# Cross attention and mixture of experts on one core: the first block only centred, its root applied behind its product, and the zero fill on ScalarE

## The chip, the cores and the metric

The kernel runs on 1 core of a Trainium2 chip. The metric is the time of one execution on the device in microseconds; of several runs the median counts. Engines are named as in the profile: PE (TensorE matmul), PEld (its weight load), DVE (VectorE), ACT (ScalarE), POOL (GpSimd), SP (SyncE).

## The reference

Input `x` has 4 x 512 = 2048 tokens of 512 values. A layernorm is followed by a first stage in which each token is sent, by its token number, to one of four context matrices; a second layernorm is followed by a mixture of 32 experts with top 4 routing and a shared expert. All is float32. What the change touches lies in the first stage:

```python
x = x + xattn(_layernorm(x), itok, ctx, ctx, ctx)
# _layernorm: (x - mean) / sqrt(var + 1e-5)
# xattn, for each of the experts e = 0..3, for the tokens whose number falls to e:
g = silu(einsum('bsd,fd->bsf', h, ctx[e]))
u = einsum('bsd,fd->bsf', h, ctx[e])
y = einsum('bsf,df->bsd', g * u, ctx[e].T)
x = x + ffn(_layernorm(x), ...)     # rmsnorm, 32 experts of 256, top 4, and a shared one
```

The three context matrices of one expert are one and the same array, so with p = h times the matrix, the gated value is silu(p) * p.

## The kernel before

**Sorting.** The tokens are sorted by expert on the chip. One-hot products on PE count and rank them (L221 to L265); `xtok` (L265) holds the token number of each sorted place. From then on work goes by blocks of 128 sorted tokens: 16 blocks of rows (`NT`), and 19 visits (`XB`), since a block that straddles two experts is visited for each. `be_i` and `bl_i` hold expert and block of each visit as integers that engines load into registers (`value_load`), `valid` masks the rows of a visit that belong to its expert.

**The plan of the first stage (`xattn`).** Each visit b goes through these steps:

- `x_block(j)` (L331): POOL requests the 128 rows of a block by an indirect DMA into `acc[:, j, :]`. These requests and the roots stand on POOL in one written order (`in_turn`).
- `x_moments` (L342, L344, L345): DVE takes mean and variance (`st`, `xmv`).
- `x_root` (L348, L351, L352): DVE adds epsilon (`ve`), POOL raises it to the power -0.5 (`xr`).
- `x_norm` (L401): DVE makes scale and bias (`rv`, L407 and L410), ACT writes the normalised rows `hn` (L426). For block 0, DVE writes the first half of the columns (L416) and ACT the second.
- `turn_block` (L438): PE transposes `hn` into `tp`, and a copy brings it to `xT` (L456 on DVE; for block 0 in halves, the first on ACT and the second on DVE, L446).
- `hold` (L385): ACT copies the visit's context matrix out of `cT` into `held`, two copies of 1024 columns (L395). Visit 0 always has expert 0 and uses `cT[:, 0]` directly.
- `up` (L459): PE forms the transposed product `pp`, 16 products of 128 columns, which the trace lists as 32 instructions (L464). For block 0 they run by input chunk c on the outside, so that they can start with the first half of `xT`.
- `gate` (L476): ACT takes silu (L478), DVE multiplies it by the product (`made`, L480) into `aT`.
- `down` (L482): PE multiplies `aT` by the same matrix, four products of 512 columns, listed as 8 instructions (L485); DVE adds the result to `acc` (L500).

`settle`, `norm` and `turn_row` then start the second layernorm of blocks that are finished; routing and the scatter of rows to `s_dram` by POOL (L652) follow, then the shared expert and the 32 experts.

**What sets the order.** A scheduler orders the instructions of each engine; `behind(a, b)` puts a behind b on its engine (with `Sync`, also behind b's end on another engine), `tc.issue_after` does it for a group. In `xattn`, rows of blocks 0, 1 and 2 are requested at once, those of block 3 behind the root of block 0, those of block 4 behind the root of block 1, and so on; blocks 8 to 15 are requested in a row behind the common root of blocks 4 to 7. `second_inputs` (norm weights, gate, shared expert, zeros for the padding rows of the output) is issued by SP when the statistics of block 7 are done, and `blanks` fills `s_dram` with zeros behind the last request.

**The head.** SP loads `tok_sb` and the first three context matrices of 1 MB (`cT`); the fourth is requested when the plan of the visits is complete (`planned`, L313). DVE makes the constants, among them `ident` (L154). POOL makes the index ramps and fills `none`, 128 x 2084 values, with zeros (L163). `turn_over(n, after_)` puts n products on PE whose results nobody reads: ten behind `xtok`, five behind the statistics of block 0.

Of the kernel before, what the change touches and what calls it, by code (L numbers as in the profile page):

```python
# [17 lines left out]
P = 128  # L18
T = 2048
D = 512  # L20
DC = D // P
GT = 4
G = T // (GT * P)
EX = 4
NT = T // P
# [41 lines left out]
def tile_xattn_moe(  # L67
# [92 lines left out]
    iota_e = const_iota([P, E], [[1, E]], "iota_e")  # L160

    spare = const_iota([P, NT, K], [[K * P, NT], [P, K]], "spare", base=NS, channel=1)
    nc.gpsimd.memset(none, 0.0)  # L163
# [203 lines left out]
    def x_registers(b):  # L367


        if b == 0:  # L370
            off[0] = 0
            regs[0] = 0, 0
            return None
        with queued(downs[-1] if downs else None):

            off[b] = nc.tensor.value_load(be_i[0:1, b : b + 1], min_val=0, max_val=min(b, EX - 1))
        with queued(adds_x[-1] if adds_x else halves[-1] if halves else None):
            dv = nc.vector.value_load(bl_i[0:1, b : b + 1], min_val=0, max_val=NT - 1)
            loaded = nc.cur_bb.bb.instructions[-1]
        with queued(reads[-1] if reads else None):  # L380
            ac = nc.scalar.value_load(bl_i[0:1, b : b + 1], min_val=0, max_val=NT - 1)
        regs[b] = dv, ac
        return loaded

    def hold(b):  # L385

        if b == 0:
            held[0] = cT[:, 0]
            return
        with queued(copies[-1] if copies else None):  # L390
            e = nc.scalar.value_load(be_i[0:1, b : b + 1], min_val=0, max_val=min(b, EX - 1))
        held[b] = ctx_pool.tile([P, DC, D], F32, tag="held", name=f"held{b}", bufs=2)
        n = DC // 2
        for h in range(0, DC, n):
            ins = nc.scalar.copy(  # L395
                held[b][:, h : h + n], cT[:, bass.ds(e, 1), h : h + n].rearrange("p o c f -> p (o c) f")
            )
            apart(ins, matrices[b + 1 :], "of experts that come later")
            copies.append(ins)

    def x_norm(b):  # L401
# [5 lines left out]
        ins = nc.vector.tensor_tensor(rv[:, 0:1], xr[:, bass.ds(dv, 1)], valid[:, b : b + 1], ALU.mult)  # L407
        apart(ins, [q for q in roots[b + 1 :] if q not in roots[: b + 1]], "of blocks that come later")
        powers.append(ins)
        scaled = nc.vector.scalar_tensor_tensor(  # L410
            rv[:, 1:2], xmv[:, bass.ds(dv, 1), 0], -1.0, rv[:, 0:1], ALU.mult, ALU.mult
        )
        hn_[b] = xpool.tile([P, D], F32, tag="hn", name="hn")
        n = D // 2 if b == 0 else 0
        if n:
            scaled = nc.vector.tensor_scalar(  # L416
                hn_[b][:, :n],
                acc[:, bass.ds(dv, 1), :n].rearrange("p o d -> p (o d)"),
                rv[:, 0:1],
                rv[:, 1:2],  # L420
                ALU.mult,
                ALU.add,
            )
            apart(scaled, loads[b + 1 :], "of blocks that come later")
            halves.append(scaled)
        ins = nc.scalar.activation(  # L426
            hn_[b][:, n:],
            acc[:, bass.ds(ac, 1), n:].rearrange("p o d -> p (o d)"),
            AF.Identity,
            bias=rv[:, 1:2],  # L430
            scale=rv[:, 0:1],
        )
        apart(ins, fronts, "of blocks that are done")
        apart(ins, loads[b + 1 :], "of blocks that come later")
        reads.append(ins)
        return scaled

    def turn_block(src, tag, name, eng, after_=None):  # L438
        t = xpool.tile([P, DC, P], F32, tag=tag, name=name)
        if eng is None:  # L440
            n, copies = DC // 2, []
            for h, copy in ((0, nc.scalar.copy), (n, nc.vector.tensor_copy)):
                tp = ps_t.tile([P, n, P], F32, tag="tp", name="tp")
                for c in range(n):
                    ins = nc.tensor.transpose(tp[:, c, :], src[:, (h + c) * P : (h + c + 1) * P], ident)
                copies.append(copy(t[:, h : h + n, :], tp))  # L446
            turns.append(ins)
            turned.append(copies[1])
            return t, copies[0]
# [6 lines left out]
        turned.append(nc.scalar.copy(t, tp) if eng is nc.scalar else nc.vector.tensor_copy(t, tp))  # L456
        return t

    def up(b, fs, after_=None):  # L459
        if fs[0] == 0:  # L460
            ups[b] = ps_m.tile([P, DC, P], F32, tag="mm", name="pp")
        pairs = [(f, c) for f in fs for c in range(DC)] if b else [(f, c) for c in fs for f in range(DC)]
        for f, c in pairs:
            ins = nc.tensor.matmul(  # L464
                ups[b][:, f, :],
                held[b][:, c, f * P : (f + 1) * P],
                xT_[b][:, c, :],
                start=(f == 0 and c == 0) if b == 0 else (c == 0),
                stop=(c == DC - 1),
                skip_group_check=(b == 0),  # L470
            )
            if after_ is not None:
                behind(ins, after_)
        ups_.append(ins)

    def gate(b):  # L476
        s = xpool.tile([P, DC, P], F32, tag="s", name="s")
        gated.append(nc.scalar.activation(s, ups[b], AF.Silu))  # L478
        aT_[b] = xpool.tile([P, DC, P], F32, tag="aT", name="aT")
        made[b] = nc.vector.tensor_tensor(aT_[b], s, ups[b], ALU.mult)  # L480

    def down(b):  # L482
        po = ps_o.tile([P, D], F32, tag="po", name="po")
# [21 lines left out]
    def xattn():  # L505
        def fetched(*js):
            for j in js:
                x_block(j)

        fetched(0, 1, 2)  # L510
        for b in range(2):
            loaded = x_registers(b)
            with tc.issue_after(loaded) if loaded is not None else nullcontext():
                st = x_moments(b)
            behind(st, scaled if b else planned)
            if not b:
                turn_over(5, st)
            x_root(b)
            fetched(3 + b)
            scaled = x_norm(b)  # L520
            if b:
                behind(reads[-1], half_)
            else:
                xT_[0], half_ = turn_block(hn_[0], "xT", "xT", None)
        hold(0)
        up(0, range(DC - 1))
        hold(1)
        xT_[1] = turn_block(hn_[1], "xT", "xT", nc.vector, ups_[0])
        up(0, range(DC - 1, DC), turns[-1])
        gate(0)  # L530
        hold(2)
        for b in range(2, GT):
            st = x_moments(b)
            behind(st, turned[b - 2])
            behind(st, scaled)
            x_root(b)
            fetched(3 + b)
        fetched(GT + 3)
        x_norm(2)
        behind(powers[-1], turned[1])  # L540
        for b in range(XB):
            j = GT * (b // 2 + 1)
            if not b:
                behind(x_moments(GT), made[0])
                x_moments(GT + 1)
            elif j < NT and b % 2 == 0:
                for i in range(j, j + GT):
                    x_moments(i)
                x_root(j, GT)
# [5 lines left out]
                hold(b + 2)  # L555
            if b + 1 < XB:
                up(b + 1, range(DC // 2))

            g, i = divmod(b - (XB - NT) - GT - 2, GT)
            if i == 0 and g >= 0:  # L560
                choose(g, ups_[-1])
            if b + 1 < XB:
                up(b + 1, range(DC // 2, DC))
                gate(b + 1)
                if not b:
                    behind(reads[-1], gated[-1])
            n = b - (XB - NT) - 2
            if n >= 0:
                row_ = turn_row(n, ups_[-1])
            if b + 2 < XB:  # L570
                xT_[b + 2] = turn_block(hn_[b + 2], "xT", "xT", nc.vector)
            if not b:
                for i in range(GT + 2, 2 * GT):
                    st = x_moments(i)
                    behind(st, turned[-1])
                x_root(GT, GT)
                fetched(*range(2 * GT, NT))
                second_inputs(st)
                blanks(loads[-1])
# [826 lines left out]
```

## Time and profile before

| What | Value |
|---|---|
| median of 3 runs | 634.53 us (633.66 to 635.23) |
| profiled execution, its own time | 634.66 us |
| its span, first to last instruction | 632.8 us |
| mean granted TensorE clock | 0.990 |
| busy PE / DVE / POOL / ACT | 606.6 / 396.8 / 249.6 / 216.6 us |
| rows requested by POOL, first and last of 16 | 10.06 and 40.81 us |
| first transposes of block 0 on PE | 16.38 us |
| product of block 1 on PE | 21.84 us |
| first `down` on PE | 25.95 us |

Times inside the profile are counted from the start of the span. The page of the profile gives busy time by engine, the span in 40 slices, the chain of work that ended last and the costliest groups. Of the other views, the timeline lists instructions in order of time, merged where alike, with the idle time ahead of them in square brackets and what ended it; the chain of waits lists start, length and holder of each piece of the chain that ended last; the windows give busy time by engine, granted clock and DMA in chosen stretches.

### The profile page before, as it was taken

Reading aid. Unit: us, or ns where it says so; the run is one execution under the profiler, and the core shown is the slowest. Engines: PE = TensorE matmul, PEld = TensorE weight load, DVE = VectorE, ACT = ScalarE, POOL = GpSimd, SP = SyncE. Lnnn points to the kernel's source line nnn. Section 1 sums busy time; section 2 is a strip of 40 time slices with the busy share of each in tenths; the row PEclk is TensorE's granted clock in tenths of the full one; section 3 lists DMA queues with packets and bytes.
Section 4 is the critical chain, followed back from the end, with each engine's and each line's share of the span. In section 5 each row is a group of like instructions: output and inputs, shape, how many; then the busy total and the mean of one; then the engine's idle time right before and its main releaser. Section 6 shows DMA issues by size and latency. Waiting matters only on the chain.

```text
span 632.8 us, 10430 instructions
## 1 busy us (share of the span) xinstructions
PE 606.6 (96%) x2962; PEld 433.8 (69%) x2962; DVE 396.8 (63%) x1113; ACT 216.6 (34%) x390; POOL 249.6 (39%) x217
## 2 busy tenths in 40 slices
PE   5999999999996999999999999999999999999993
PEld 2777767777542444467687688858868886888882
DVE  7645457666734812675578577766766778677860
ACT  2444766665321000122233333332232333233330
POOL 4451111366673565424233235143332423434323
PEclk9999999999997999999999999999999999999998
DMA  7489992326273596799989998997999799999434
GB/s 253 147 316 416 412 415 100 136 103 221 102 270 118 175 392 210 212 299 291 299 209 273 275 258 199 276 249 155 288 257 256 168 266 250 246 251 217 52 48 56
DMA packets 104450, 144.55 MB, mean 228 GB/s; under 512 B 21184, under 2 KB 58048, under 8 KB 101824
## 3 DMA queue, kind: packets, MB, share of 16 engines
q1 hardware_dynamic: 86400, 101.54, 54.6%
q0 software_dynamic: 17984, 42.26, 27.5%
q8 instruction: 26, 0.43, 0.3%
q14 instruction: 40, 0.33, 0.2%
HBM read 79.05 MB, written 66.22 MB: 230 GB/s over the span
## 4 chain that ended last, share of the span: by engine, by line
PE 73%; POOL 8%; issue 7%; DVE 4%; DMA 4%; SPq 2%; another core or an unknown queue 1%; ACT 0%; POOLq 0%; DVEq 0%
PE pg L1068 17%; PE pu L1068 17%; PE po L1103 16%; PE pp L464 5%; POOL s_dram L652 4%; PE po L485 4%; PE pp_x L1150 3%; DMA acc<-in_x,xtok 3%; PE po L870 2%; PE pg L855 2%; PE po L1176 2%; SPq L940 2%; PE pu L855 2%; POOL rs L618 1%
## 5 line engine op out<-in xcount | busy, mean ns | idle before, releaser
L1040 POOL DMA_INDIRECT out<-eo,to_all x64 | 104.4, 1631 | 220.2 <-DVE eo L1109 87.2
L1068 PE MATMUL pg<-xT,w 128*128 128x256 f32 (+2 forms) x512 | 135.4, 377 | 0.0
L1106 ACT ACTIVATE eo<-po,wt 128x256 f32<-128x256 f32 x124 | 58.6, 475 | 172.8 <-PE po L1103 127.4
L1068 PE MATMUL pu<-xT,w 128*128 128x256 f32 (+2 forms) x512 | 114.0, 376 | 0.0
L1068 PEld LDWEIGHTS pg<-xT,w 128*128 128x128 f32 x512 | 96.6, 190 | 18.5 <-issue 6.2
L1068 PEld LDWEIGHTS pu<-xT,w 128*128 128x128 f32 x512 | 97.3, 190 | 11.5
L652 POOL DMA_INDIRECT s_dram<-h,slot x64 | 62.2, 971 | 35.2 <-issue 16.6
L464 PEld LDWEIGHTS pp<-xT,held 128*128 128x128 f32 x576 | 66.8, 192 | 7.6 <-issue 5.2
L464 PE MATMUL pp<-xT,held 128*128 128x128 f32 x576 | 68.2, 276 | 0.8 <-DVE st_b L611 0.6
L485 PE MATMUL po<-cT,aT 128*128 (+1 forms) x152 | 68.4, 592 | 0.0
L991 DVE STREAM_TRANSPOSE xT<-z 128x1024 f32<-128x1024 f32 x32 | 65.1, 2036 | 0.0
L1109 DVE SCALAR_TENSOR_TENSOR eo<-po,wt,eo 128x256 f32<-128x256 f32 x93 | 45.0, 484 | 18.6 <-PE po L1103 12.0
L1075 DVE TENSOR_TENSOR aT_r<-s,pu 128x256 f32<-128x256 f32 (+2 forms) x64 | 26.2, 414 | 43.0 <-PE pu L1068 37.2
L485 PEld LDWEIGHTS po<-cT,aT 128*128 128x128 f32 x152 | 27.4, 190 | 27.3 <-issue 27.3
L1001 ACT ACTIVATE xT<-xT,nwq 128x256 f32<-128x256 f32 x64 | 29.0, 500 | 44.6 <-DVE xT L991 32.7
L1086 DVE TENSOR_TENSOR t_r<-w,t_r 128x256 f32<-128x256 f32 x62 | 26.3, 424 | 28.0 <-PE po L1103 27.9
L618 POOL TENSOR_TENSOR rs<-rs,mhalf 128x2 f32<-128x2 f32 x16 | 11.3, 705 | 72.7 <-DVE rs L617 72.7
L1103 PE MATMUL po<-w,aT_r 128*128 128x256 f32 x124 | 39.8, 402 | 0.0
L395 ACT COPY held<-cT 128x1024 f32 x36 | 36.0, 1046 | 10.2 <-DVE valid L312 9.9
L1103 PE MATMUL po<-t_r,s_r 128*128 128x256 f32 x124 | 37.8, 386 | 0.3 <-DVE s_r L1093 0.3
L1103 PE MATMUL po<-t_r,aT_r 128*128 128x256 f32 x124 | 37.5, 384 | 0.0
L870 PE MATMUL po<-shw,aT_s 128*128 128x512 f32 x64 | 32.1, 640 | 1.5 <-issue 1.2
(203 smaller groups left out, 763.5 us busy)
## 6 DMA issues: line engine op xcount, KB each, us to landing
w<-in_w SPq DMA_DIRECT2D x192, 256.0 KB
s_dram<-none SPq DMA_DIRECT2D x1, 20840.0 KB
z<-s_dram SPq DMA_DIRECT2D x128, 128.0 KB
h_dram<-h SPq DMA_DIRECT2D x4, 1042.0 KB
cT<-in_ctxT SPq DMA_DIRECT2D x4, 1024.0 KB
out<-none SPq DMA_DIRECT2D x1, 1024.0 KB
s_dram<-h,slot POOLq DMA_INDIRECT x64
out<-eo,to_all POOLq DMA_INDIRECT x64
```

Source lines behind the costliest of these rows:

```text
L395: ins = nc.scalar.copy(held[b][:, h : h + n], cT[:, bass.ds(e, 1), h : h + n].rearrange("p o c f -> p (o c) f"))
L464: ins = nc.tensor.matmul(ups[b][:, f, :], held[b][:, c, f * P : (f + 1) * P], xT_[b][:, c, :], start=(f == 0 and c == 0) if b == 0 else (c ...
L485: ins = nc.tensor.matmul(po, aT_[b][:, f, :], cT[:, bass.ds(off[b], 1), f, :].rearrange("p o f -> p (o f)"), start=(f == 0), stop=(f == DC ...
L652: put = nc.gpsimd.indirect_dma_start(out=table, out_offset=bass.IndirectOffsetOnAxis(ap=index, axis=0), in_=src, in_offset=None,)
L870: ins = nc.tensor.matmul(po, aT[:, f, i * P : (i + 1) * P], w2t[:, f, :], start=(f == 0), stop=(f == IC - 1))
L991: ins = nc.vector.transpose(xT.rearrange("p c (r b) -> p r c b", b=SQ), z.rearrange("p r (a c) -> p r c a", c=DC))
L1001: nc.scalar.mul(xT[:, c, :], xT[:, c, :], nwq[:, c : c + 1])
L1040: put = nc.gpsimd.indirect_dma_start(out=out, out_offset=bass.IndirectOffsetOnAxis(ap=dst, axis=0), in_=eo, in_offset=None, bounds_check=T ...
L1068: last_up = nc.tensor.matmul(ps, w13t[:, c, f * P : (f + 1) * P], xT[:, c, :n], start=(c == 0), stop=(c == DC - 1))
L1103: return nc.tensor.matmul(ps, L[i], R[i], start=first_, stop=True, skip_group_check=True)
L1106: nc.scalar.mul(eo[i][:, j, :], ps, wt[:, i : i + 1])
L1109: return nc.vector.scalar_tensor_tensor(eo[i][:, j, :], ps, wt[:, i : i + 1], eo[i][:, j, :], ALU.mult, ALU.add)
```

## The change

Three things are changed in the first stage; what is computed stays the same.

- Block 0 is only centred: `x_centre` subtracts the mean, first half of the columns on DVE, second half on ACT with the negated mean as bias. Its root is made later. `x_scale` multiplies it by `valid`, and `gate(0)` applies it as a scale in silu and in the product. For that the root must lie along partitions, so the product of block 0 is formed with the rows held in PE and the matrix moving: four products of 512 columns, with tokens on partitions. The gated rows are then transposed (`turn_first`) and copied to `aT` by DVE. Both halves of `xT` of block 0 are copied by ACT. Two idle products follow the statistics of block 0, not five.
- The zero fill of `none` is an ACT multiplication by 0.
- The rows of block 3 are requested behind those of block 2, ahead of the root of block 0.

With these come new places in the order: the statistics of blocks 4 to 7 are all behind the copy of `xT` of block 2; those of block 3 are behind the gated product of block 0; the third copy of `held` is behind `hn` of block 1 and the fourth behind the silu of block 1.

```diff
-    nc.gpsimd.memset(none, 0.0)
+    nc.scalar.mul(none.rearrange("p j w -> p (j w)"), ones16[:, 0:1].to_broadcast([P, NB * RW]), 0.0)
...
+    def x_centre():
+        regs[0] = 0, 0
+        off[0] = 0
+        neg = xpool.tile([P, 2], F32, tag="rv", name="rv", bufs=3)
+        nc.vector.tensor_scalar(neg[:, 0:1], xmv[:, 0, 0:1], -1.0, None, ALU.mult)
+        hn_[0] = xpool.tile([P, D], F32, tag="hn", name="hn")
+        n = D // 2
+        scaled = nc.vector.tensor_scalar(hn_[0][:, :n], acc[:, 0, :n], xmv[:, 0, 0:1], None, ALU.subtract)
+        halves.append(scaled)
+        reads.append(nc.scalar.activation(hn_[0][:, n:], acc[:, 0, n:], AF.Identity, bias=neg[:, 0:1]))
+        first_.append(neg)
+        return scaled
+
+    def x_scale():
+        ins = nc.vector.tensor_tensor(first_[0][:, 1:2], xr[:, 0:1], valid[:, 0:1], ALU.mult)
+        powers.append(ins)
+        return ins
...
-            for h, copy in ((0, nc.scalar.copy), (n, nc.vector.tensor_copy)):
+            for h in (0, n):
...
-                copies.append(copy(t[:, h : h + n, :], tp))
+                copies.append(nc.scalar.copy(t[:, h : h + n, :], tp))
...
+        for f in fs:
+            for c in range(DC) if b else [f]:
+                if b:
+                    ps, left, right = ups[b][:, f, :], held[b][:, c, f * P : (f + 1) * P], xT_[b][:, c, :]
+                else:
+                    ps, left, right = ups[b].rearrange("p f t -> p (f t)"), xT_[b][:, c, :], cT[:, 0, c, :]
+                ins = nc.tensor.matmul(ps, left, right, start=(c == 0), stop=(c == DC - 1))
...
     def gate(b):
...
+        by = first_[0][:, 1:2]
+        gated.append(nc.scalar.activation(s, ups[b], AF.Silu, scale=by))
+        made[b] = nc.vector.scalar_tensor_tensor(s, ups[b], by, s, ALU.mult, ALU.mult)
+        first_.append(s)
+
+    def turn_first(after_):
+        aT_[0] = turn_block(first_[1].rearrange("p f t -> p (f t)"), "aT", "aT", nc.vector, after_)
...
+        fetched(0, 1, 2, 3)
+        st = x_moments(0)
+        behind(st, planned)
+        turn_over(2, st)
+        scaled = x_centre()
+        xT_[0], half_ = turn_block(hn_[0], "xT", "xT", None)
+        x_root(0)
+        loaded = x_registers(1)
+        with tc.issue_after(loaded):
+            st = x_moments(1)
+        behind(st, scaled)
+        x_root(1)
+        fetched(4)
+        scaled = x_norm(1)
+        behind(reads[-1], half_)
+        behind(x_scale(), scaled)
+        halves.append(scaled)
         up(0, range(DC - 1))
         hold(1)
         xT_[1] = turn_block(hn_[1], "xT", "xT", nc.vector, ups_[0])
         up(0, range(DC - 1, DC), turns[-1])
-        gate(0)
         hold(2)
+        behind(copies[2], reads[-1])
         for b in range(2, GT):
             st = x_moments(b)
-            behind(st, turned[b - 2])
-            behind(st, scaled)
+            behind(st, scaled if b == 2 else made[0])
             x_root(b)
             fetched(3 + b)
+            if b == 2:
+                scaled = x_norm(2)
+                behind(powers[-1], turned[-1])
+                gate(0)
+                behind(made[0], scaled)
         fetched(GT + 3)
...
                 up(b + 1, range(DC // 2, DC))
+                if not b:
+                    turn_first(ups_[-1])
                 gate(b + 1)
                 if not b:
                     behind(reads[-1], gated[-1])
+                    behind(copies[3], gated[-1])
+                    behind(powers[-1], turned[-1])
+                    behind(made[1], turned[-1])
...
             if not b:
-                for i in range(GT + 2, 2 * GT):
+                for i in range(GT, 2 * GT):
                     st = x_moments(i)
                     behind(st, turned[-1])
                 x_root(GT, GT)
```

More of the change, by code (lines that the diff above doesn't have):

```diff
@@ L367, in x_registers @@
     def x_registers(b):
[L370 to L373, printed above, removed]
         with queued(downs[-1] if downs else None):
@@ L385, in hold @@
     def hold(b):
-        if b == 0:
-            held[0] = cT[:, 0]
-            return
         with queued(copies[-1] if copies else None):
@@ L399, in hold @@
             copies.append(ins)
+    first_ = []
+    def x_centre():
[14 more added lines that the diff above has]
+        return ins
     def x_norm(b):
@@ L413, in x_norm @@
         hn_[b] = xpool.tile([P, D], F32, tag="hn", name="hn")
[L414 to L425, printed above, removed]
         ins = nc.scalar.activation(
-            hn_[b][:, n:],
-            acc[:, bass.ds(ac, 1), n:].rearrange("p o d -> p (o d)"),
+            hn_[b],
+            acc[:, bass.ds(ac, 1), :].rearrange("p o d -> p (o d)"),
             AF.Identity,
@@ L445, in turn_block @@
                     ins = nc.tensor.transpose(tp[:, c, :], src[:, (h + c) * P : (h + c + 1) * P], ident)
-                copies.append(copy(t[:, h : h + n, :], tp))
+                copies.append(nc.scalar.copy(t[:, h : h + n, :], tp))
             turns.append(ins)
             turned.append(copies[1])
-            return t, copies[0]
+            return t, copies[1]
         tp = ps_t.tile([P, DC, P], F32, tag="tp", name="tp")
@@ L461, in up @@
             ups[b] = ps_m.tile([P, DC, P], F32, tag="mm", name="pp")
[L462 to L473, printed above, removed]
+        for f in fs:
[5 more added lines that the diff above has]
+                ins = nc.tensor.matmul(ps, left, right, start=(c == 0), stop=(c == DC - 1))
+                if after_ is not None:
+                    behind(ins, after_)
         ups_.append(ins)
@@ L477, in gate @@
         s = xpool.tile([P, DC, P], F32, tag="s", name="s")
-        gated.append(nc.scalar.activation(s, ups[b], AF.Silu))
-        aT_[b] = xpool.tile([P, DC, P], F32, tag="aT", name="aT")
-        made[b] = nc.vector.tensor_tensor(aT_[b], s, ups[b], ALU.mult)
+        if b:
+            gated.append(nc.scalar.activation(s, ups[b], AF.Silu))
+            aT_[b] = xpool.tile([P, DC, P], F32, tag="aT", name="aT")
+            made[b] = nc.vector.tensor_tensor(aT_[b], s, ups[b], ALU.mult)
+            return
+        by = first_[0][:, 1:2]
[4 more added lines that the diff above has]
+        aT_[0] = turn_block(first_[1].rearrange("p f t -> p (f t)"), "aT", "aT", nc.vector, after_)
     def down(b):
@@ L508, in fetched @@
                 x_block(j)
[L510 to L525, printed above, removed]
+        fetched(0, 1, 2, 3)
[15 more added lines that the diff above has]
+        halves.append(scaled)
         up(0, range(DC - 1))
@@ L529, in xattn @@
         up(0, range(DC - 1, DC), turns[-1])
-        gate(0)
         hold(2)
+        behind(copies[2], reads[-1])
         for b in range(2, GT):
             st = x_moments(b)
-            behind(st, turned[b - 2])
-            behind(st, scaled)
+            behind(st, scaled if b == 2 else made[0])
             x_root(b)
             fetched(3 + b)
+            if b == 2:
[3 more added lines that the diff above has]
+                behind(made[0], scaled)
         fetched(GT + 3)
-        x_norm(2)
-        behind(powers[-1], turned[1])
         for b in range(XB):
             j = GT * (b // 2 + 1)
[L543 to L546, printed above, removed]
+            if b and j < NT and b % 2 == 0:
                 for i in range(j, j + GT):
```

## The prediction

> **What bounds the kernel now.** First the page, parts 1 and 2. TensorE (PE) is busy nearly everywhere, so the time is the moment at which its unbroken work begins, plus that work, plus its pauses.
>
> ```profile
> PE 606.6 (96%) x2962; PEld 433.8 (69%) x2962; DVE 396.8 (63%) x1113; ACT 216.6 (34%) x390; POOL 249.6 (39%) x217
> PE   5999999999996999999999999999999999999993
> ```
>
> The change touches the first 46 us, so next the chain of waits over that stretch (start, us, what).
>
> ```profile
> 1.67 1.85 DVE ident L154
> 3.52 0.12 DVE ge L226 x3
> ...
> 12.82 7.16 DMA acc<-in_x,xtok
> 19.98 0.02 issue
> 20.00 0.71 DVE st_a L344
> ...
> 23.46 0.56 POOL xr L352
> ...
> 25.51 3.48 DMA acc<-in_x,xtok
> ...
> 30.69 1.03 POOL xr L352
> ...
> 35.76 6.83 DMA acc<-in_x,xtok
> ...
> 44.66 3.81 PE pp L464 x32
> ```
>
> Up to 44.66 it is not a chain of PE work. It is a chain of row requests: the rows of block 2 land at 19.98, their statistics release the root and the request behind it, and so on through blocks 7 and 11; only from 44.66 on does the chain stay on PE (`pp`, `po`). The head is, in the timeline of all engines:
>
> ```profile
> 1.54 1.99 DVE L154 TENSOR_SCALAR ident<-iota_q,row_b 128x128 f32<-128x128 f32 x1
> 1.59 1.85 POOL L163 MEMSET none<- 128x2084 f32 x1
> 14.91 0.58 POOL L352 TENSOR_TENSOR xr<-ve,mhalf 128x1 f32<-128x1 f32 x1 [1.15 <-DVE ve L351]
> 15.52 0.16 DVE L407 TENSOR_TENSOR rv<-xr,valid 128x1 f32<-128x1 f32 x1 [0.70 <-POOL xr L352]
> 15.72 0.16 DVE L410 SCALAR_TENSOR_TENSOR rv<-xmv,rv 128x1 f32<-128x1 f32 x1
> 16.38 0.44 PE L445 MATMUL tp<-ident,hn 128*128 128x128 f32 x2 [0.65 <-DVE hn L416]
> 21.10 0.69 DVE L456 COPY xT<-tp 128x512 f32<-128x512 f32 x1
> ```
>
> The reader should see three things: `ident` ends (3.53) when the POOL memset ends (3.44); the root stands between the statistics of block 0 and its transposes; and the copy of `xT` of block 1, which releases the product of block 1 at 21.84, runs behind the statistics of block 2. From 20.41 to 44.44 PE has no pause over 0.15 us, then one of 0.22.
>
> **The change, part by part.**
>
> Zero fill. `tri` (same size, written as f16) took 0.28 us; `ident` took 1.99 beside the memset. Without it I give `ident` 0.3 to 0.4, so it ends near 1.95. The first `ge` started at 2.42 (its tokens are there) and ended only at 3.53; with its own 0.15 it ends at 2.58. Gain 0.95 for all that hangs on it: `xtok` 9.59 to 8.64, requests 0, 1, 2 and the last context matrix (behind `planned`) alike. From below it is 0, if `ident` is slow for another reason. On ScalarE the fill is 2084 columns; the 1024-column copy takes 1.05, so 2.1 us, from 2.23 to 4.4, in an idle stretch that lasts to 12.18: cost 0; it could only cost if it ran past 11.
>
> Block 0 centred only. Statistics end at 14.63. Before, `ve`, root and two `rv` bring `hn` to 15.91. After, one negated mean (0.16, with 0.04 between) puts both halves at 14.87: 1.04 earlier. ScalarE must be free then: it copied `held` three times until 15.12, and the third copy now goes behind `hn` of block 1. With the 0.95 the transposes start near 14.4 instead of 16.38. Three idle products fewer (0.25 each) end before that; cover nothing, cost nothing.
>
> Both copies of block 0's `xT` on ScalarE: 0.37 each, before 0.37 and 0.42 in parallel with the second transposes. Neutral on PE; it takes 0.4 us from between the two statistics instructions of block 1 on DVE.
>
> Product of block 0: 8 instructions of 512 columns (3.44 us for 8 in the `po` rows) for 32 of 128 (3.57): 0.13 less. `silu` with a scale and the product with three inputs: taken at the 0.60 and 0.69 of their rows, both under the product of block 1.
>
> New: the gated rows must be turned. Four transposes behind the product of block 1: 0.44 on PE. Then a copy on DVE before `down(0)`: from the first transpose to the copy's start 0.64 (48.30 to 48.94), copy 0.69, release 0.05: 1.38. PE has 0.86 of other transposes to cover it, so 0.5 us of pause. Before, `aT` was ready at 23.31 for 25.95.
>
> Request 3 goes out at 13.1 instead of 15.68. No wait ends with its landing (DVE starts the statistics of block 3 at 21.71 without idling), so 0. Roots 0 and 1 queue behind it on POOL; root 0 is needed by `silu` near 20, five microseconds of cover.
>
> DVE order. Before, the statistics of block 3 followed the copy of `xT` 1 at once. After, they are behind the two `rv` of block 2 and the gate product of block 0; those of blocks 4 to 7 are behind the copy of `xT` 2, which is itself behind the copy of the turned rows.
>
> **The walk.** Block 1 lands 0.95 earlier, 15.5; its `hn`, 2.65 after its statistics before, 0.4 less now, is at 17.7, transposes 18.55, PE free at 19.9. But the product of block 1 needs the copy of `xT`, which I take to stay behind the statistics of block 2, as now: landing 19.98 - 0.95 = 19.03, plus the 1.86 that now lies between landing and product, 20.9. So PE gains 0.95 here, not 2.0, and pauses 1.0 first. Then 3.7 to the first new transpose (24.6), plus 1.38: `down(0)` starts at 25.95. It started at 25.95. The lead is spent.
>
> The row chain: product of block 2's `rv` and gate 0, 21.0 to 22.0; statistics 3, `ve`, root 3 at 23.1 (before 23.46); requests 6 and 7 0.4 earlier, block 7 lands at 28.6. But DVE, from the copy of the turned rows at 25.23, owes this: that copy 0.65, `rv` of block 3 0.35, copy 0.6, gate product 0.6, four statistics 2.65, aggregates 0.5: 5.35, so it ends near 30.5 (before 29.93) and `ve` of blocks 4 to 7 stands between 30.4 and 30.95 (before 30.44; a register load of 0.5 stood ahead of it, and may not now). I take 0.3 later, nearer the row as it is. Requests 8 to 15 and the second inputs (released by the statistics of block 7) move with it, so 44.66 moves by +0.3, and PE has nothing to set against it.
>
> The sum: 634.66 (profiled execution: span 632.8 and 1.9 around it) + 0.3 = 635.0; the median is 0.13 below that execution, so 634.8. Ends of this case: if landing 2 gains 1.6 rather than 0.95, -0.6, 633.9; if it gains nothing because the context matrix, asked for earlier too, is ahead of it again, 0.95 later, +1.25, 635.8.
>
> A rule that speaks against the change stands in the Trainium skill, "TensorE: Matmul & The Clock Gate", section "What's actually happening": an idle window of about 3.4 us halves PE's clock. The row first:
>
> ```profile
> 189.00:196.00 7.00, 1.28 (x3) 0.19 (x3) 0.14 (x1) 0.30 (x2) 3.45 (x4) 0.86 0.47 182
> 196.00:198.00 2.00, 2.00 (x4) 0.78 (x5) 0.87 (x3) 1.24 (x1) 0.00 (x0) 0.50 0.00 0
> ```
>
> (stretch, its length, busy of PE, PEld, DVE, ACT, POOL, granted clock, DMA.) A pause of 4.74 us cost half the clock; pauses of 0.72 and 0.65 in the head left it at 1.00. My new pauses are 0.6 and 1.0, nearer the second row: cost 0; the upper bound is half clock over the product of block 0, +1.7. By the page's window the cost would be 0 too, though five idle products now become two.
>
> "DMA: Bandwidth & Descriptors", section "Queues, rings and completion order", says that an engine takes turns between queues. By that the rows of block 2 would need, as an estimate from its rule, 0.7 more than the 3.48 of an undisturbed request, landing at 17.0. The trace has 19.98: 7.16 after the request, while DMA moved 391 GB/s at 16 to 17. I go by the trace; by the page the lead would live.
>
> **Rivals.**
> - The lead survives. If block 2 lands well before PE needs it, or the copy of `xT` 1 goes ahead of its statistics, PE keeps 0.95, at most 2.0 - 0.44 = 1.55; if DVE then also ends its statistics by 29.7, 44.66 moves by the same. 632.6 to 633.6. For: request 3 and the earlier landing free POOL. Against: the DVE sum above holds whichever way the copy goes.
> - The late pause changes. 188.74 to 196 is 4.74 us of pause plus some 2.5 lost at clock 0.50, and it ends when a semaphore reaches ScalarE after POOL's last scatter (193.36). New spacing of POOL against PE can shorten or lengthen it by a quarter to a half of these 7.2: 1.8 to 3.6 either way, 630.9 to 632.7 or 636.3 to 638.1.
> - Slower: the rows of block 2 land later than before. The 1 MB matrix is asked for 0.95 earlier, now on top of the last packets of matrix 2, and block 2 queues behind it. `down(0)` then waits for landing, copy, product, transposes and copy in a row, so each us is paid in full on top of 1.25. It decides from a landing at 20.6; the queue already lets block 2 wait 3.7 us (7.16 - 3.48), and I allow 1.5 more: +1.9 to +2.75, 636.4 to 637.3.
>
> **How the numbers follow.** 0.3% is 1.9 us, about what a measurement of this kernel can tell from no change. Forecast 0.40, all within. Lead survives 0.15, a third of it beyond 1.9 us. Late pause 0.27, 0.15 faster and 0.12 slower. Late landing 0.18, slower. Faster 0.05 + 0.15 = 0.20, slower 0.30, within 0.50. The likeliest case alone is 633.9 to 635.8; the range of 632.0 to 637.5 leaves out the outer parts of the late pause, some 0.17.
>
> **What would show it.** Right: `ident` under 0.5 us, transposes near 14.4, product of block 1 near 20.9 behind a DVE copy, `down(0)` near 26 with a pause before it, `ve` of blocks 4 to 7 within 0.5 of 30.44, and the first product with no pause after it at 44.2 to 45.2. Wrong: `ident` still long; product of block 1 near 20.0; the DMA that ends at 42.59 more than 1 us away; another pause at 189.

## The result, and the profile after

The kernel after took 635.15 us (median of 20 runs, 633.86 to 640.25), the kernel before, on the same chip, 633.90 (20 runs, 632.24 to 635.23). The ratio is 1.0026 with a 95% interval of 1.0016 to 1.0037: slower, by a little less than the 0.3% that the prediction calls no change. The medians lie 1.25 us apart, the means 1.7, since the runs of after reach further up. The profiled execution took 634.48 us, its span is 632.7.

The page's first two parts, of after:

```profile
PE 606.5 (96%) x2939; PEld 431.4 (68%) x2939; DVE 395.4 (62%) x1113; ACT 219.6 (35%) x393; POOL 245.1 (39%) x216
PE   5899999999996999999999999999999999999994
```

PE is as busy as before. POOL gave up 4.5 us and ACT took 3.0, which moves nothing by itself. The chain of waits over the head, of after (start, us, holder; DVEq is DVE's sequencer, here loading registers):

```profile
2.40 0.34 DVE ge L226 x3
...
11.92 7.38 DMA acc<-in_x,xtok
...
19.31 0.70 DVE st_a L344
...
20.22 0.14 DVEq L374
...
20.45 0.19 DVEq L374
...
20.74 0.15 DVE ve L351
20.90 0.17 DVEq L374
...
21.15 0.19 DVEq L374
...
21.44 0.70 DVE xT L459
...
22.19 3.84 PE pp L471 x32
26.03 0.45 PE tp L455 x4
...
26.50 0.70 DVE aT L459
...
27.25 3.70 PE po L494 x8
...
45.83 3.81 PE pp L471 x32
```

Three readings. From 22.19 on this chain is PE's but for one copy of the turned rows at 26.50, where before it was still a chain of row requests up to 44.66. The product of block 4 starts at 45.83 instead of 44.66, so 1.17 us are lost in the head. And between the statistics of block 2 and the copy of `xT` 1 stand two register loads (L374), about 0.5 us each with the gaps inside them, that were not there before.

Three rows of the timeline of after answer to those shown of before:

```profile
1.54 0.28 DVE L154 TENSOR_SCALAR ident<-iota_q,row_b 128x128 f32<-128x128 f32 x1
2.03 1.94 ACT L163 ACTIVATE none<-ones 128x2084 f32<-128x2084 f16 x1
14.72 0.44 PE L448 MATMUL tp<-ident,hn 128*128 128x128 f32 x2
```

`ident` fell from 1.99 to 0.28, the fill takes 1.94 on ACT, and the transposes of block 0 start 1.66 earlier. POOL's next index ramp waits 2.40 us for the fill, until 4.04, which costs nothing: POOL's first row request waits for DVE until 9.16 in any case. The change does what it says; the gain is gone by 22.19.

### The profile page after: what moved, and what is told of

Its sections match the earlier page's. It is cut to its first block, busy times and chain, and to the rows that moved or that the text cites. A ratio compares the mean times of both kernels' runs of the same rounds, so it can differ in the third digit from the quotient of the medians.

```text
span 632.7 us, 10386 instructions
## 1 busy us (share of the span) xinstructions
PE 606.5 (96%) x2939; PEld 431.4 (68%) x2939; DVE 395.4 (62%) x1113; ACT 219.6 (35%) x393; POOL 245.1 (39%) x216
## 4 chain that ended last, share of the span: by engine, by line
PE 77%; POOL 6%; issue 6%; DMA 3%; DVE 3%; SPq 2%; another core or an unknown queue 1%; ACT 0%; POOLq 0%; DVEq 0%
PE pg L1081 17%; PE pu L1081 17%; PE po L1116 16%; PE pp L471 6%; PE po L494 6%; POOL s_dram L665 4%; PE pp_x L1163 3%; PE pg L868 3%; PE pu L868 3%; PE po L883 2%; PE po L1189 2%; SPq L953 2%; DMA acc<-in_x,xtok 1%; POOL rs L631 1%
## 5 line engine op out<-in xcount | busy, mean ns | idle before, releaser
L1053 POOL DMA_INDIRECT out<-eo,to_all x64 | 102.3, 1599 | 221.8 <-DVE eo L1122 94.6
```

Source lines behind the costliest of these rows:

```text
L1053: put = nc.gpsimd.indirect_dma_start(out=out, out_offset=bass.IndirectOffsetOnAxis(ap=dst, axis=0), in_=eo, in_offset=None, bounds_check=T ...
```

## The experiments

The theories, as they are named in the expectations. **A**: the register loads of blocks 2 and 3 now stand ahead of the copy of `xT` 1 and cost about 1.04 us, which PE carries to the end. **B**: the chain of row requests still binds. **C**: the pause of PE near 189 makes the difference. **D** and **E** came with later runs: that pause belongs to the chip, and the clock falls behind the long pause ahead of the product of block 1. Twelve runs followed, of seven new kernels (before, after, e1 and e6 ran again), in four groups on four chips, here called the second to the fifth; each has its own runs of before beside it (medians 625.36 for the first four, 624.09 for the next four, 634.26 for the next three, 624.85 for the last). The number of the first chip is not on record, so the fourth may be the same one.

| Kernel | statistics of block 2 | product of block 1 | first `down` | product of block 4 | end of PE | ratio to before, 95% |
|---|---|---|---|---|---|---|
| before, first chip | 20.00 | 21.84 | 25.95 | 44.66 | 622.70 | |
| after, first chip | 19.31 | 22.19 | 27.25 | 45.83 | 623.46 | 1.0026 [1.0016, 1.0037] |
| e1 loads early | 19.42 | 21.17 | 26.23 | 44.87 | 614.12 | 1.0003 [0.9992, 1.0013] |
| e2 fill alone | 19.41 | 21.53 | 25.64 | 44.53 | 613.87 | 0.9986 [0.9976, 0.9996] |
| e3 request alone | 20.36 | 22.12 | 26.23 | 44.55 | 613.65 | 0.9995 [0.9986, 1.0003] |
| e4 POOL fill | 20.46 | 23.34 | 28.40 | 47.50 | 616.64 | 1.0043 [1.0029, 1.0056] |
| e5 before again | 20.21 | 21.96 | 26.08 | 44.62 | 613.88 | |
| e6 fill and requests | 20.02 | 21.77 | 25.88 | 44.20 | 613.35 | 0.9989 [0.9981, 0.9998] |
| e7 copy first | 20.14 | 20.28 | 25.34 | 44.12 | 613.35 | 0.9996 [0.9987, 1.0005] |
| e8 change again | 19.52 | 22.39 | 29.07 | 48.03 | 617.19 | 1.0049 [1.0035, 1.0064] |
| e9 pause filled | 19.84 | 22.71 | 27.77 | 46.57 | 625.40 | 1.0023 [1.0011, 1.0034] |
| e10 change third | 19.90 | 22.78 | 27.84 | 46.58 | 625.27 | 1.0029 [1.0016, 1.0041] |
| e11 loads early again | 19.57 | 21.32 | 26.38 | 45.10 | 624.05 | 1.0014 [1.0001, 1.0026] |
| e12 best again | 19.73 | 21.48 | 25.59 | 43.91 | 613.08 | 0.9987 [0.9973, 1.0000] |

Starts and ends are those of the one profiled execution of each, the ratios those of all its runs. Behind the end of PE another 7.8 to 10.3 us pass until the end of the span, without order by kernel (10.1 in before, 9.2 in after, 8.0 in e5, 10.0 in e2). That is a scatter larger than the change, so the times of single profiled executions are not set against each other here, only their starts.

### e1: the register loads early

In after, `halves.append(scaled)` tells the register loads of blocks 2 and 3 to stay behind the scale of block 1. This kernel drops it:

```diff
         behind(x_scale(), scaled)
-        halves.append(scaled)
         up(0, range(DC - 1))
```

> The changed kernel, except that DVE's register loads for blocks 2 and 3 queue behind the centring of block 0 again, as in the kernel before, and no longer behind the scale of block 1. Theory A (the two register loads that stand between the statistics of block 2 and the copy of xT 1 cost 1.04 us, and PE carries that to the end): the product of block 1 starts at 21.15 instead of 22.19, down(0) at 26.2, the product of block 4 at 44.8 instead of 45.83, and the time is 1.0 us under the changed kernel, within 0.3 us of the kernel before (ratio 1.000 to 1.0005). Theory B (the chain of row requests binds: statistics of blocks 4 to 7 behind the copies): the product of block 1 moves as under A, but the product of block 4 stays at 45.3 or later and less than half of the 1 us reaches the end (ratio 1.001 to 1.002). Theory C (the difference arises in the late pause at 190 us): the head moves, the time stays as in the changed kernel (ratio 1.002 to 1.003).

The chain of waits, of e1:

```profile
19.42 0.70 DVE st_a L344
...
20.44 0.69 DVE xT L459
...
21.17 3.84 PE pp L471 x32
...
25.48 0.70 DVE aT L459
...
26.23 3.70 PE po L494 x8
...
44.87 3.81 PE pp L471 x32
```

No DVEq stands between the statistics and the copy, and every start lies within 0.1 us of what A gave. From the statistics of block 2 to the product of block 1 it is 1.75 us here and in e11, and 2.87 or 2.88 in after, e4, e8, e9 and e10: five executions with the loads there, two without, and no overlap. In e1 DVE makes these loads from 16.39 to 17.69, before the rows of block 2 are there (19.40). With the loads back in earlier gaps the change costs little or nothing (1.0003 here, 1.0014 in e11). A stands for the start of the products. In the times it is less sharp: on the one chip that ran both, e10 and e11, the intervals of the two ratios overlap.

### e2, e3, e4: the parts by themselves

e2 is before with the fill on ScalarE (the one changed line of the diff), e3 is before with request 3 ahead of root 0, e4 is after with the fill back on POOL.

```diff
# e3, against before
-        fetched(0, 1, 2)
+        fetched(0, 1, 2, 3)
...
-            fetched(3 + b)
+            if b:
+                fetched(3 + b)
```

> The kernel before with one part of the change: ScalarE writes the zeros. Theory A (a late landing of block 2's rows binds the kernel before, and the fill moves all requests): ident takes 0.3 us instead of 1.99, request 0 at 9.16, block 2 lands near 19.3 instead of 19.98, the product of block 4 starts 0.4 to 0.7 us earlier than 44.66, and the time falls by that (ratio 0.9989 to 0.9994): faster than both kernels. Theory B: block 2's landing moves, but its gain is eaten by a later wait before 44.66: ratio 0.9997 to 1.0003. Theory C: the head gains and the late pause decides: anything within 0.002 of 1, without relation to the start of the product of block 4.

> The kernel before with one part of the change: rows of block 3 requested behind those of block 2, ahead of the root of block 0. Theory A: nothing waits for those rows; root 0 starts 0.2 us later (15.1), transposes of block 0 at 16.55, the landing of block 2 (19.98) and the product of block 1 (21.84) stay within 0.1, ratio 0.9997 to 1.0003. Rival: the earlier request takes bandwidth from block 2 or the last matrix, block 2 lands 0.3 to 0.8 us later and the product of block 4 moves as much: ratio 1.0005 to 1.0013.

> The changed kernel with the zero fill back on POOL. Theory A: ident takes 1.99 again, request 0 goes out at 10.06 instead of 9.16, block 2 lands 0.5 to 0.7 later than 19.31 and every later step up to the product of block 4 (45.83) moves by that: 46.3 to 46.5, ratio to the kernel before 1.0028 to 1.004. Theory B (the DVE order sets the changed kernel, not the landing): the product of block 4 stays within 0.2 of 45.83, ratio as the changed kernel. Theory C: the head moves and the time does not.

The timeline of e4, the two rows that the fill decides:

```profile
1.54 1.99 DVE L154 TENSOR_SCALAR ident<-iota_q,row_b 128x128 f32<-128x128 f32 x1
2.47 1.16 DVE L226 TENSOR_SCALAR ge<-tok_sb 128x16 f16<-128x16 int32 x3
```

With the memset on POOL `ident` is back at 1.99 us, as in before and e5; without it, it is 0.28. The fill is the part of the change that pays: alone it is faster than before (the interval of e2 ends at 0.9996), and its interval lies under that of after. Its gain shrinks on the way, as B says: against before on the first chip 0.64 at request 0 (9.42 against 10.06), 0.59 at the statistics of block 2, 0.11 at `ve` of blocks 4 to 7 (30.33 against 30.44), 0.13 at the product of block 4. But the ratio of 0.9986 is 0.9 us, more than B allows and more than those 0.13, and the profiled execution of e2 (625.91) was 1.3 above its median; where the time of its other runs was gained is not shown. Request 3 alone is worth nothing that can be told from no change, the prediction's 0. In e3 block 2 landed 0.36 later than in before on the first chip and 0.15 later than in e5, where A had it within 0.1; the product of block 4 did not move with it. In e4 the product of block 4 moved by 1.67 against after where A had 0.5 to 0.7: the rows of block 2 came 1.15 later, all of it reached PE, and the row requests, released late by DVE, added a pause of 0.51. The 0.5 to 0.7 fits the first chip, where block 2 landed 0.69 earlier in after than in before; on e4's own chip the statistics of block 2 lie 1.04 apart between e4 and e1 and 0.95 between e3 and e2.

### e5: before once more

> The kernel before, unchanged, for a profile on a second chip. On the first chip PE paused at 188.74 to 196.0 and ran at half clock; four kernels on another chip showed no pause there. Theory D (the late pause belongs to the chip or the session and is worth the whole difference between 634 and 625): no PE pause over 0.3 us between 180 and 200, PE's end near 614, product of block 4 at 44.66 as on the first chip, within 0.15. Rival: the pause is there in the kernel before and was only absent in the four variants; then 188.7 to 196 shows it again.

The windows of e5, and then the row of the timeline of after that ends the pause near 189:

```profile
189.00:196.00 7.00, 7.00 (x19) 3.10 (x18) 6.04 (x24) 2.67 (x3) 5.47 (x6) 1.00 0.53 207
```

```profile
197.18 0.48 PE L696 MATMUL pl<-ident,lT 128*128 128x128 f32 x1 [6.27 <-ACT lT L690]
```

The same kernel runs through 189 to 196 with PE busy 7.00 of 7.00 us at full clock, where on the first chip it idled and then ran at 0.50. So D holds: the long pause was in none of the nine profiles on the second, third and fifth chips, and in all five on the first and fourth (3.8 to 6.3 us, in e9 to e11 with shorter ones ahead of it), whatever the kernel. Whether the chip or the session makes it can't be told, since each group ran at one time on one chip. From the product of block 4 to the end of PE it is 569.10 to 569.34 us in e1 to e8 and e12, and 577.6 to 579.0 where the pause is. Two things follow. Where the pause is absent, what a kernel loses by the product of block 4 arrives at the end of PE in full. And the pause with its half clock is worth about 9 us, many times the change, with no part in it. Why it is there in some groups was not found.

### e6 and e12: the fill, and requests 3 to 7 earlier

```diff
# against before, with the fill on ScalarE
-        fetched(0, 1, 2)
+        fetched(0, 1, 2, 3)
...
-            fetched(3 + b)
+            if b:
+                fetched(4, 5)
...
-            fetched(3 + b)
-        fetched(GT + 3)
+            if b == 2:
+                fetched(6, 7)
```

> The kernel before with two things: the zero fill on ScalarE, and the row requests of blocks 3 to 7 each moved ahead of a root on POOL (order on POOL: requests 0 to 3, root 0, root 1, requests 4 and 5, root 2, requests 6 and 7, root 3). Block 0 is normalised as before. Theory B (the chain of row requests binds until block 4, and the fill's 0.95 is lost along it): request 7 goes out some 2 us earlier, its rows land near 26.5 instead of 28.9, epsilon of blocks 4 to 7 at 28.5 to 29.3 instead of 30.3, the pause of 0.40 ahead of the product of block 4 is gone, that product at 44.1 instead of 44.53; ratio to before 0.9980 to 0.9985. Rival: the earlier rows only meet the context matrices on the DMA queues, and DVE's own work sets epsilon of blocks 4 to 7 (30.2 or later); product of block 4 stays at 44.5 and the ratio at that of the fill alone, 0.9986.

The timeline of e6:

```profile
29.30 0.17 DVE L351 TENSOR_SCALAR ve<-xmv 128x4 f32<-128x4 f32 x1 [0.52 <-DVE xmv L345]
44.20 3.73 PE L464 MATMUL pp<-xT,held 128*128 128x128 f32 x32
```

Request 7 goes out at 23.26 (25.51 in before), epsilon of blocks 4 to 7 is ready 1.25 earlier than in e5, no idle time stands in brackets ahead of the product of block 4, and PE is the bound from the product of block 1 on, 22.43 us ahead. From the product of block 1 to that of block 4 it is 22.82 in before, 22.66 in e5 and 23.00 in e2, so B stands as a description of them, for 0.2 to 0.6 us; in e3, where the product of block 1 came at 22.12, it is 22.43 too, and nothing is lost. The ratio of 0.9989 is no better than the fill alone: 0.42 us at the product of block 4 is under 0.1%.

> The kernel before with the zero fill on ScalarE and the requests of blocks 3 to 7 each ahead of a root, a second time. Theory B: PE without a pause from the product of block 1 on, product of block 4 at 44.1 to 44.3 (44.62 in before), epsilon of blocks 4 to 7 near 29.3, no half clock between 14 and 46; ratio 0.998 to 0.9995. Rival: the gain of the first time (0.9989) was the chip's scatter, and the ratio is 0.9996 or more.

On the fifth chip the product of block 4 is at 43.91, again exactly 22.43 behind that of block 1, and the ratio is 0.9987. This version beat before both times; against e2 it can't be told apart.

### e7: the copy ahead of the statistics

```diff
# against e1
-        fetched(4)
+        fetched(4, 5)
...
-            behind(st, scaled if b == 2 else made[0])
+            behind(st, turned[-1] if b == 2 else made[0])
...
-            fetched(3 + b)
...
+                fetched(6, 7)
...
-        fetched(GT + 3)
```

> The kernel after with three things: the register loads of blocks 2 and 3 not held behind the scale of block 1 (as in the run in which they are early), the copy of xT of block 1 ahead of the statistics of block 2 on DVE, and requests 4 and 5 ahead of root 2's place, 6 and 7 together. This is the case in which the lead of block 0 can survive. Theory A (what is gained ahead of the product of block 1 is spent on the turned rows): product of block 1 at 20.6 to 20.8 instead of 21.17, down(0) at 25.6 to 25.8 instead of 26.23, of which 0.43 are transposes and some 0.35 a wait for their copy; product of block 4 at 44.3 to 44.4; ratio 0.9985 to 0.9995, no better than the fill alone. Rival (the lead survives): product of block 1 near 20.0 and product of block 4 at 43.5 or before; ratio 0.9975 or less.

This is the prediction's case in which the lead survives, made on purpose. The product of block 1 starts at 20.28, 1.68 ahead of e5, and the first `down` at 25.34, 0.74 ahead: the turned rows took 0.94. At the product of block 4 0.50 is left, behind a pause of 0.19, because epsilon of blocks 4 to 7 waits for DVE to copy the turned rows first (29.99). The gain was larger at block 1 than A gave, and spent as A said; the ratio doesn't tell it from before.

### e8, e9, e10, e11: the change again, and the clock

e8 and e10 are after unchanged, e11 is e1 unchanged, e9 is after with five idle products in the pause ahead of the product of block 1:

```diff
         up(0, range(DC - 1, DC), turns[-1])
+        turn_over(5, ups_[-1])
```

> The kernel after, unchanged, beside the others. Theory A (the loss lies in the head, 1.17 us at the product of block 4, and has nothing to do with the pause at 189): ratio 1.0017 to 1.0026, product of block 4 at 45.7 to 45.9, and no pause at 189. Rival C (the late pause made the difference on the first chip): ratio within 0.9995 to 1.0008 where that pause is absent.

The ratio is 1.0049, above A's range and far from C's. The windows of e8 (stretch, its length, busy PE, PEld, DVE, ACT, POOL, granted clock, DMA share, GB/s) and its timeline of PE:

```profile
19.63:23.04 3.41, 1.50 (x7) 0.67 (x7) 2.28 (x7) 1.26 (x3) 1.56 (x2) 1.00 0.20 68
23.20:26.40 3.20, 3.20 (x17) 3.20 (x16) 0.99 (x4) 0.29 (x1) 1.56 (x3) 0.50 0.28 82
```

```profile
22.39 5.47 PE L471 MATMUL pp<-xT,held 128*128 128x128 f32 x32 [1.92 <-DVE xT L459]
```

The clock is halved from 23.04 to 26.45, 3.41 us, and the product of block 1 takes 5.47 instead of 3.84. That is 1.63, close to the prediction's upper bound of 1.7 for a half clock, which it set at 0; it fell on the next product rather than on that of block 0. With a new pause of 0.37 ahead of the product of block 4 it makes the 2.0 by which e8 is behind after from block 1 to block 4.

> The kernel after with five more idle products on PE (128x512, f16, some 0.26 us each, results read by nobody) behind the last products of block 0, in the pause ahead of the product of block 1. The dependences that release that product stay. Theory E (in most executions of the kernel after, the long pause ahead of the product of block 1 makes the granted clock fall to 0.50 for some 3.3 us, which adds 1.6 us to that product; in the first profile of after it did not, in the third chip's it did): with the pause filled the clock stays at 1.00 from 20 to 28, the product of block 1 starts at 22.2 to 22.4 and takes 3.84, product of block 4 at 45.7 to 46.1, ratio 1.0015 to 1.0028, and its runs have no tail above 1.5 us over their median. Rival (the clock's fall has nothing to do with the pause): half clock in the same place, ratio as that of the kernel after beside it.

> The kernel after, unchanged, beside the one with the pause filled. Theory E: pause of 1.5 to 2.0 us ahead of the product of block 1; if the profile shows 0.50 in the granted clock after it, that product takes 5.4 to 5.5 instead of 3.84; ratio 1.004 to 1.005 where most executions fall, 1.0026 where few do, and a spread of its runs about twice that of the one with the pause filled. Rival: ratio within 0.0007 of the filled one's.

> The kernel after with the register loads of blocks 2 and 3 not held behind the scale of block 1, a second time, beside the others. Theory A with E: the loads are both the 1.04 us and what makes the pause long enough for the clock; pause ahead of the product of block 1 0.4 to 0.6, clock 1.00 from 20 to 28, product of block 1 at 21.1 to 21.3, product of block 4 at 44.8 to 45.0, ratio 0.9992 to 1.0015. Rival: ratio above 1.002, so that something else of the change costs as well.

E is not settled by these runs. In e9 the stretch from 20 to 28 stays at full clock, but so it does in e10, where the pause of 1.93 is not filled: a pause of that length alone doesn't halve the clock, and e9 doesn't show that filling it helped. In e9 a half clock came earlier, from 16.09 to 19.50, on the product of block 0 (4.49 us for six instructions instead of 2.79). There it cost little, because PE then waits for the copy of `xT` 1 anyway: that product starts at 22.71, as in e10 at 22.78. The ratios, 1.0023 and 1.0029, lie 0.0006 apart, as the rival of e10 had it, and the spread of e10's runs (3.0 us) is not twice that of e9's (3.4).

How little PE is busy in any 3.41 us that begin after 16.2 separates the kernels: 1.48 to 1.52 at the least in after, e4, e8 and e10, 2.07 to 2.16 in e1 and e11, and 2.8 or more in the rest. A half clock behind such a stretch was seen once in the first four, in e8. The Trainium skill, "TensorE: Matmul & The Clock Gate", section "What's actually happening", says that the clock is judged over a free-running window of 3413 ns. The traces agree, and they show where these windows lie: within each trace the steps of the granted clock are whole multiples of 3.413 us apart. In e9 they come at 16.09, 19.50, 193.59 and 203.82, that is 0, 1, 52 and 55 windows from the first. Counted back from the half clock of e10 (193.42 to 203.66), one of its windows is 19.34 to 22.75, and in e12, counted back from a step at 616.74, one is 12.59 to 16.00. The windows of e10, e9 and e12:

```profile
19.34:22.75 3.41, 1.51 (x6) 0.68 (x6) 1.75 (x5) 1.56 (x2) 0.98 (x2) 1.00 0.27 82
193.42:203.66 10.24, 6.38 (x9) 2.32 (x9) 2.91 (x17) 2.83 (x4) 2.60 (x3) 0.50 0.26 102
```

```profile
12.68:16.09 3.41, 1.87 (x9) 0.66 (x8) 1.35 (x5) 1.58 (x3) 1.80 (x3) 1.00 0.88 270
16.09:19.50 3.41, 3.41 (x6) 1.35 (x6) 1.42 (x6) 1.38 (x3) 1.57 (x2) 0.50 0.65 256
```

```profile
12.59:16.00 3.41, 1.72 (x7) 0.41 (x5) 1.76 (x6) 2.12 (x3) 1.83 (x3) 1.00 0.87 278
```

On windows so placed PE was busy for 1.50 us in e8 and 1.87 in e9, and the clock fell; it was busy for 1.51 in e10, 1.72 in e12 and 1.85 in after, and the clock stayed. So neither the pause, nor PE's busy time in the window, nor the place of the window tells e8 from e10, and what does was not found. How often after is hit stays open too: five of the six runs of e8 lie at 627.0 to 628.5 and one at 625.43, but only one of them has a trace.

e11's ratio is 1.0014, and e1's 1.0003. Both intervals hold values of 1.0001 to 1.0013, so the rest of the change is worth between nothing and 0.8 us of loss.

## Why the prediction was right and wrong

The forecast, little change because the lead of block 0 is spent before the fourth block, was right in kind, and its total of 634.8 is 0.35 us from the median. Part of that is luck: it starts from the median of 3 runs of before, 634.53, and the 20 runs have 633.90. The measured difference, 1.25 us against 0.3 forecast, was not right: one term was missing, by which there was no lead left to spend. The product of block 1 came 0.35 late instead of 0.94 early.

- **The fill**: `ident` 0.28 (0.3 to 0.4 forecast), request 0 0.90 earlier (0.95), 1.94 on ACT (2.1). Right.
- **Landing of block 2**: 0.69 earlier, not 0.95. Block 0's rows came only 0.41 earlier, although asked for 0.90 earlier. The rule weighed on the DMA queues, in the Trainium skill, "DMA: Bandwidth & Descriptors", section "Queues, rings and completion order", would by the prediction's estimate have had block 2 of before at 17.0; the row (7.38 from request to landing, 7.16 before) decided.
- **The step that failed**: "plus the 1.86 that now lies between landing and product". It became 2.90 (19.29 to 22.19). The sum moved the copy with the statistics but gave 0 to DVE's register loads, which the added line `halves.append(scaled)` holds until the scale of block 1 is done. So 20.9 became 22.19: 0.26 from the landing and 1.04 from this. e1 shows it. The prediction did see a register load of 0.5 ahead of `ve` of blocks 4 to 7, and left it out here. As to its price, the Trainium skill, "DMA: Bandwidth & Descriptors", section "Latency and other measured facts", gives about 600 ns as the floor of a `tensor_load`. The chain shows less here: 0.52 and 0.54 us for each load with its register work.
- **The turned rows**: from the product of block 1 to the first `down` 5.06 against 5.05 forecast (4.11 before), the pause 0.35 against 0.5. Right, and 5.06 again in e1, e4, e7, e9, e10 and e11; 6.68 in e8, with the half clock.
- **The row chain**: `ve` of blocks 4 to 7 at 31.89, not 30.7, since the copy of the turned rows, with which DVE's work for it begins, came at 26.50, not 25.23. But PE was later still, and the chain hardly binds in after: the product of block 4 starts 3.60 behind the start of the `down` ahead of it, where 3.44 is the undisturbed step (34.79 to 38.23 in after) and before had 3.82.
- **The sum**: at the product of block 4, 0.35 (block 1) + 0.95 (turned rows) - 0.13 (the wait ahead of it fell from 0.38 to 0.16, and the step behind the first `down` grew by 0.09) = 1.17. Forecast: -0.94, +0.94 and +0.3.
- **Rivals**: the late landing didn't come. The late pause did not make the loss: from the product of block 4 to the end of PE after is 0.41 shorter than before on the first chip. The lead can survive only in another order (e7), and of its 1.68 there 0.50 is left at the product of block 4.
- **The clock**, costed at 0: right in the first profile, wrong in that of e8. The bound was right, and the rows that it was chosen by, pauses of 0.72 and 0.65, were shorter than the pause of 1.57 that came.

## What to carry to other kernels

When a step is moved ahead on an in-order engine, list everything that is tied to it, register loads too, and put each into the sum at its price where the engine's next waiter stands: here two loads of half a microsecond undid a lead of one. A lead is worth only what no later step must pay back, so walk it to the point from which the bound engine never pauses again, and read the sum there. And where a change opens a pause on PE, put a half clock behind it into the sum as a possible cost, here 1.63 us: among the pauses of 1.2 to 1.9 us seen here neither their length nor PE's busy time around them told whether it would come.

## What was not expected of the hardware

- A half clock of 3.4 us came with PE busy for 1.50 and 1.87 of the 3.41 us ahead of it, in e8 and e9, and did not come with 1.51 in e10. The Trainium skill, "TensorE: Matmul & The Clock Gate", section "What's actually happening", speaks of an idle window; here no wholly idle window was needed.
- The same kernel takes 624 us on one chip and 634 on another, and nearly the whole difference is the long pause of PE with the half clock around it, between 189 and 204.
- `ident` takes 1.98 to 1.99 or 0.28 us, by whether POOL's memset runs beside it, in fourteen profiles without exception. The Trainium skill, "SBUF — State Buffer", section "Who interferes with whom", states an exclusive lock on a port that DVE and POOL share, which fits.
